# A window-attention layer and a dynamic convolution on one core: how the first rounds load their vectors and fold their weights

## The chip, the cores and the metric

The kernel runs on 1 core of one Trainium2 chip, in one launch. The metric is the device time of one execution in microseconds (us). Five engines work beside each other, each through its own queue in program order: TensorE (PE, matrix products into the banks called PSUM), VectorE (DVE), ScalarE (ACT), GpSimd (POOL), and SyncE (SP), which here only issues transfers (DMA). ACT can issue transfers too.

## The reference, cut to what matters

The input is 16 images of 192 channels, 56 x 56, in float32. Layer 0 is a shifted-window attention block (windows of 7 x 7, 6 heads of 32) with an MLP, layer 1 a 3 x 3 depthwise convolution whose taps are computed from the image's own mean.

```python
# layer 0
h = ln(x, norm1_g, norm1_b)                 # over the 192 channels of a pixel
win = windows(roll(h, (-3, -3)))            # (B*64, 49, 192)
q, k, v = split(win @ qkv_w + qkv_b)
attn = softmax(q * SCALE @ k.T + bias[rel] + mask)
x1 = x + unroll(attn @ v @ proj_w + proj_b)
y = gelu(ln(x1, norm2_g, norm2_b) @ fc1_w + fc1_b) @ fc2_w + fc2_b
x = x1 + y
# layer 1
t = relu(bn(x.mean((2, 3)) @ w1.T))
wt = (t @ w2.T + b2).reshape(B * 192, 1, 3, 3) * MASK   # four taps are left
out = depthwise_conv(x, wt) + bias
```

The normalisation's scale and shift need not be applied to the pixels. With g, b and the mean over channels, `ln(x) @ W + c = rstd * (x @ W') + (b @ W + c)`, where W' is W with its rows times g, and then less its column mean. The kernel computes W' (it is called centred) and `b @ W` (the shift) once, for the qkv weights and for the fc1 weights. This is called folding.

## The kernel before

**Tiling.** An image is cut into 4 strips (NU) of two bands of 7 rows, one band in partitions 0 to 63 and one in 64 to 127; the 192 channels are three groups (G) of 64. 16 images make S = 64 strips, and the index s of a strip is called a step here. A strip is two times 392 (UT) pixels wide. Weights are held twice, for the two halves of the partitions, where the contraction is over 64 channels.

**Rounds.** The program is written as rounds r from -2 to S + 2. A round works on several steps at once: scores and values of step r, q and k of step r + 1, the attention-weighted sum and the projection of step r - 1, the first MLP layer of step r - 2, the second of step r - 3, and pieces of the convolution of an image that is finished. In the first rounds (r < 3, called early) the statistics of the first normalisation come from a full product (`full_deviations`, PE L385), so that each is ready at once; later they go by a transfer to memory and back (`deviations`).

**Order.** No engine's order is written by hand. Each operation is handed to a planner (`Plan.add`) with its engine, a guessed duration, the keys that it reads and writes, a lag if it is a transfer, and sometimes a due time (`by`). PE's operations keep the order in which they are added. For the other engines the planner simulates the program with those guesses and takes, whenever an engine is free, the operation that can start first, and of those the one that is due first. So a guess, a key or a due time that is changed can move instructions on every engine but PE. Eight transfers at most are in flight: each issue, on SP or on ACT, waits for the one eight places before it.

**What the change touches.** Lines are those of the kernel before.

- `small_loads` (L1184): 14 transfers for the seven vectors of 192 numbers (`vecs`, one element to a partition, for both halves), six for the qkv biases (`qkb`, `bv`), one for `fc1_b` (`f1b`), all on ACT's queue, 21 in all.
- `load_qkv` (L1236): ten transfers on SP that put the qkv weights in the tile `wqkv`, in an order of columns that gives chunks of 128 (q of four heads, k of four heads, q and k of the other two) and then v.
- `fold_weights` (L1290): for n = 0 (qkv) or 1 (fc1), in this order on PE: the shift `b @ W` as products with one moving column (L1302), and the means (L1320); then on DVE the centring in place (L1335).
- `fold_qkv` (L1355): shifts in five chunks, then the biases `bq`, `qbs`, `km` of q and k and `bv` of v.
- `fold_proj` (L1374): v's bias is not added to v. Since the shares of a row sum to 1, it passes through to the projection, and this function multiplies `bv` by the projection's weights (PE L1382, L1386, one column each) and adds `proj_b`, giving `pbt`, which `biased_rows` (L749) adds to x on ACT.
- `statistics(n, s)` (L291): squares of the strip (ACT L297), then three groups added into one for x and for the squares (POOL L304, L306).
- `full_deviations` (L379): PE L385, ACT L393, DVE L400, ACT L407 and L411 give 1 / std of every pixel, `rb`.
- `scaled1(s)` (L418): x times `rb`, sorted into windows, in the tile `xs1` (POOL L427, L438). `queries_keys` (PE L471) and `values` (PE L665) read it.
- `queries_keys` evacuates q on ACT (L484, L508), k on DVE and ACT (L495, L518, L527). `scores` is PE L551 and DVE L577, L588. `values` copies out on ACT (L680), and eight transfers (L689) turn the copies.
- `weighted` is PE L718, with the o copies on ACT (L745) and DVE (L747). `projection` is PE L789 and L775, added to x by DVE (L817). `first_layer` is PE L828.
- `biases_of_positions` (L1418): seven transfers `relrows` (L1441) within memory, and four that read them back (L1455); DVE L1470 adds them to the masks.

The early rounds as they are added:

```python
        if r == -2:
            ...
            load(1, -80.0, 5.0)
            scaled_g()
            statistics(0, 0)
            full_deviations()
            fold_qkv()
        ...
        if r == 0:
            fold_fc1()
            fold_taps()
        if r == 1:
            fold_proj()
```

Of the kernel before, what the change touches and what calls it, by code (L numbers as in the profile page):

```python
# [14 lines left out]
G = 3  # L15
# [125 lines left out]
def tile_swin_then_dynamic_conv(  # L141
# [70 lines left out]
    tt = sb("tt", 128, 2, 48, TL)  # L212
    pt = sb("pt", 128, 2, 48, TL)
# [28 lines left out]
    qkb = sb("qkb", 128, 3)  # L242
# [6 lines left out]
    bv = sb("bv", 128, 2)  # L249
    pbt = sb("pbt", 128, G)  # L250
# [40 lines left out]
    def statistics(n, s):  # L291

        xv = rows(s).rearrange("p g r c -> p g (r c)")
        add(
            "ACT",
            1.2,
            lambda: nc.scalar.activation(sq, xv, AF.Square),  # L297
            X(s),
            ["sq"],
        )  # L300
        for k, src, keys in ((0, xv, X(s)), (1, sq, ["sq"])):
            f = fold[:, n, k]
            def go(src=src, f=f):
                nc.gpsimd.tensor_tensor(f, src[:, 0], src[:, 1], ALU.add)  # L304
            def go2(src=src, f=f):
                nc.gpsimd.tensor_tensor(f, f, src[:, 2], ALU.add)  # L306
            add("POOL", 1.0, go, keys, [("f", n, k)])
            add("POOL", 1.0, go2, keys + [("f", n, k)], [("f", n, k)])
# [108 lines left out]

    def scaled1(s):  # L418

        xv = rows(s)  # L420
        d = xs1
# [3 lines left out]
        for g in range(G):  # L425
            def go(g=g):
                nc.gpsimd.tensor_tensor(  # L427
# [5 lines left out]
            add("POOL", 0.95, go, X(s) + RB(0), [("xs1", g)])  # L433
        last = d[:, :, nf * N : UT].rearrange("p g (r c) -> p g r c", c=WS)
        rg = rv.rearrange("p (o r) c -> p o r c", o=1)
        for lo, hi, at in ((0, WS - SHIFT, IMG - WS + SHIFT), (WS - SHIFT, WS, 0)):
# [7 lines left out]
            add("POOL", 0.35, go, X(s) + RB(0), [("xs1", "w", lo)])  # L444

    def XS1(s):
        return [("xs1", g) for g in range(G)] + [
            ("xs1", "w", 0),
            ("xs1", "w", WS - SHIFT),
        ]  # L450
# [12 lines left out]
    def queries_keys(s, parts):  # L463
        d = xs1
        for i in parts:
# [14 lines left out]
            add("PE", 1.98, product, XS1(s) + ["wqkv"], [pk])  # L480
# [23 lines left out]
            else:  # L504
                for ab in range(2):
                    for h, lo, hi in ((0, 0, QL), (1, QL, N)):
# [8 lines left out]
                        add("ACT", 0.4, go, [pk, "qb", "qpad"], [("q2", ab, h)])  # L515
                for h in range(2):
# [8 lines left out]
                    add("ACT", 0.71, go, [pk, "qb", "mask2"], [("kbd2", 0, h)])  # L525
# [9 lines left out]
                    add("DVE", 0.58, go, [pk, "qb", "mask2"], [("kbd2", 1, h)])  # L535
# [110 lines left out]
    def values(s):  # L646

        n = 8 * G * TL  # L650
# [7 lines left out]
        for m in range(G):  # L658
            p, pk = bank()

            def product(m=m, p=p):
                for g in range(G):
                    for wh in range(2):
                        for ab in range(2):
# [3 lines left out]
                                xs1[P(ab), g, wh * 4 * N : (wh + 1) * 4 * N],  # L668
# [5 lines left out]
            add("PE", 0.99, product, XS1(s) + ["wqkv"], [pk])  # L674
            for b, n in ((0, TL), (1, N - TL)):
                def keep(m=m, p=p, b=b, n=n):
# [3 lines left out]
                    nc.scalar.copy(dst, src[:, :, :, TL * b : TL * b + n])  # L680
# [888 lines left out]
    for r in range(-2, S + 3):  # L1569
# [41 lines left out]
        if r == 1:  # L1611
            fold_proj()
# [131 lines left out]
```

## Time and profile before

| what | value |
|---|---|
| median of 3 runs | 2756.68 us (2754.64, 2756.68, 2763.43) |
| the profiled execution | 2756.27 us, its span 2754.5 us |
| busy share of the span | PE 98%, DVE 71%, ACT 61%, POOL 56% |
| first MLP product (L828) starts | 128.79 us |
| bytes moved by DMA | 239.62 MB, mean 87 GB/s |

The profile is of one execution. Its span runs from the first instruction to the last; the time of the execution is 1.8 us longer. A row of the profile names a line, an engine, the tiles written and read, and the count. In float32 a product on PE shows as two passes, so that L385, which is two instructions, shows as four. [...]

### The profile page before, as it was taken

How to read it: one execution, taken by the hardware profiler on the slowest of the kernel's cores; microseconds unless marked ns; L12 is line 12 of the kernel's file. 1: busy time of each engine (PE TensorE's matmuls, PEld its weight loads, DVE VectorE, ACT ScalarE, POOL GpSimd, SP SyncE). 2: the span in 40 equal slices, each digit the busy share in tenths (PEclk: the TensorE clock that was granted, in tenths of full speed). 3: DMA queues.
4: the chain of work that ended last, by engine and by line, in shares of the span. 5: the costliest groups of instructions: out<-in, count | busy, mean ns of one | idle time of the engine just before them, and what ended most of it. 6: DMA issues, size and time to landing. Idle time of an engine off the chain costs nothing.

```text
span 2754.5 us, 78133 instructions
## 1 busy us (share of the span) xinstructions
PE 2709.1 (98%) x32869; PEld 1670.9 (61%) x32869; DVE 1958.3 (71%) x3452; ACT 1682.4 (61%) x2788; POOL 1554.8 (56%) x1436
## 2 busy tenths in 40 slices
PE   7899999999999999999999999999999999999998
PEld 5566566566566566566566566566566566666654
DVE  5765876768677676876767777676876767767674
ACT  3656666656666566666666666575666666566553
POOL 5555565565565565565655655655655655655532
PEclk9899999999999999999999999999999999999999
DMA  6522353343424344253353423344253343533231
GB/s 128 111 63 60 72 119 71 80 101 91 105 67 100 73 99 94 68 127 67 74 109 87 109 67 90 77 104 92 67 122 74 76 109 70 115 79 71 62 78 52
DMA packets 146840, 239.62 MB, mean 87 GB/s; under 512 B 39432, under 2 KB 104888, under 8 KB 146488
## 3 DMA queue, kind: packets, MB, share of 16 engines
q1 hardware_dynamic: 141400, 233.40, 37.9%
q8 instruction: 258, 4.23, 0.7%
q10 hardware_dynamic: 5088, 1.22, 0.3%
q14 instruction: 94, 0.77, 0.1%
HBM read 66.81 MB, written 38.98 MB: 38 GB/s over the span
## 4 chain that ended last, share of the span: by engine, by line
PE 97%; DVE 1%; POOL 1%; ACT 0%; issue 0%; DMA 0%; ACTq 0%; DVEq 0%; POOLq 0%
PE ps L866 28%; PE ps L828 28%; PE ps L471 14%; PE ps L665 7%; PE ps L551 5%; PE ps L718 5%; PE ps L789 5%; PE ps L775 2%; PE ps L320 2%; PE ps L1302 0%; DVE sq L962 0%; POOL xs L427 0%; DVE hid L1142 0%; PE ps L1320 0%; PE ps L385 0%
## 5 line engine op out<-in xcount | busy, mean ns | idle before, releaser
L866 PE MATMUL ps<-hid,wf 128*64 128x392 f32 x4608 | 774.0, 494 | 0.3 <-issue 0.3
L828 PE MATMUL ps<-xs,wf 64*128 64x392 f32 x4608 | 769.5, 489 | 0.0
L828 PEld LDWEIGHTS ps<-xs,wf 64*128 64x128 f32 x4608 | 445.9, 187 | 312.6 <-issue 0.9
L866 PEld LDWEIGHTS ps<-hid,wf 128*64 128x64 f32 x4608 | 331.2, 137 | 406.6 <-issue 369.6
L304 POOL TENSOR_TENSOR fold<-sq 128x392 f32<-128x392 f32 x128 | 130.6, 1021 | 699.8 <-PE ps L320 690.0
L611 POOL TENSOR_TENSOR e<-e,tot 128x784 f32<-128x784 f32 x192 | 324.1, 1699 | 206.7 <-DVE tot L606 197.2
L840 ACT ACTIVATE hid<-ps,b1f 128x784 f32<-128x784 f32 x384 | 342.1, 913 | 141.2 <-PE ps L828 138.8
L471 PE MATMUL ps<-xs,wqkv 64*128 64x392 f32 x2304 | 407.6, 504 | 12.0 <-POOL xs L438 9.4
L1142 DVE SCALAR_TENSOR_TENSOR y<-x,wt,y 128x770 f32<-128x770 f32 x270 | 313.9, 1182 | 66.1 <-ACT y L1004 45.2
L471 PEld LDWEIGHTS ps<-xs,wqkv 64*128 64x128 f32 x2304 | 220.2, 190 | 178.4 <-issue 19.4
L593 POOL TENSOR_TENSOR e<-e,top 128x784 f32<-128x784 f32 x192 | 283.1, 1503 | 35.8 <-DVE top L588 35.8
L484 ACT ACTIVATE q<-ps,qbs 128x400 f32<-128x400 f32 (+1 forms) x128 | 68.3, 588 | 327.9 <-PE ps L471 327.9
L605 DVE TENSOR_REDUCE tot<-e 128x16 f32<-128x784 f32 x192 | 182.1, 948 | 109.9 <-ACT e L600 109.8
L745 ACT COPY o<-ps 32x392 f32<-32x392 f32 x512 | 243.8, 476 | 16.7 <-PE ps L718 3.0
L622 DVE STREAM_TRANSPOSE tt<-e 128x512 f32<-128x512 f32 x384 | 245.8, 684 | 3.0 <-POOL e L611 1.5
L756 ACT ACTIVATE x<-x,pbt 128x392 f32<-128x392 f32 x192 | 105.3, 612 | 204.8 <-POOL xs L438 204.8
L341 DVE TENSOR_TENSOR m<-ps,m 128x196 f32<-128x196 f32 (+1 forms) x64 | 23.2, 362 | 275.6 <-ACT m L334 275.5
L427 POOL TENSOR_TENSOR xs<-x,rb 128x343 f32<-128x343 f32 x192 | 186.7, 1001 | 39.0 <-DMA rb<-rsd 17.7
L456 POOL TENSOR_TENSOR xs<-x,rb 128x392 f32<-128x392 f32 x192 | 193.4, 1039 | 25.2 <-DMA rb<-rsd 25.2
L665 PE MATMUL ps<-xs,wqkv 64*64 64x196 f32 x4608 | 206.0, 328 | 0.7 <-DVE rb L400 0.3
L304 POOL TENSOR_TENSOR fold<-x 128x392 f32<-128x392 f32 x128 | 131.9, 1031 | 121.3 <-DVE x L817 92.9
L577 DVE TENSOR_TENSOR e<-ps,bt 128x784 f32<-128x784 f32 x192 | 175.2, 967 | 11.8 <-ACT hid L840 6.8
(128 smaller groups left out, 3649.8 us busy)
## 6 DMA issues: line engine op xcount, KB each, us to landing
pt<-tt SPq DMA_DIRECT2D x256, 192.0 KB
vb<-kbd SPq DMA_DIRECT2D x488, 96.0 KB
x<-in_x_dram SPq DMA_DIRECT2D x112, 294.0 KB
out_dram<-y SPq DMA_DIRECT2D x135, 196.0 KB
pt<-tt SPq DMA_DIRECT2D x256, 96.0 KB
rb<-rsd SPq DMA_DIRECT2D x118, 196.0 KB
out_dram<-y SPq DMA_DIRECT2D x45, 154.0 KB
x<-in_x_dram SPq DMA_DIRECT2D x16, 168.0 KB
```

Source lines behind the costliest of these rows:

```text
L304: nc.gpsimd.tensor_tensor(f, src[:, 0], src[:, 1], ALU.add)
L456: nc.gpsimd.tensor_tensor(xs2[:, g], xv[:, g], rb[:, 1], ALU.mult)
L471: nc.tensor.matmul(p[:, ab, 0:UT], lhs_qk(ab, g, i), d[P(ab), g, 0:UT], start=(g == 0), stop=(g == G - 1), tile_position=(64 * ab, 0),)
L593: nc.gpsimd.tensor_tensor(ev, ev, top[j].broadcast_to([128, 16, N]), ALU.subtract)
L611: nc.gpsimd.tensor_tensor(ev, ev, tot[j].broadcast_to([128, 16, N]), ALU.mult)
L622: nc.vector.transpose(tt[:, kb, 16 * j : 16 * j + 16], src)
L665: nc.tensor.matmul(p[P(wh), ab, 0 : 4 * N], wqkv[P(ab), g, 2 * DIM + 64 * m : 2 * DIM + 64 * m + 64], xs1[P(ab), g, wh * 4 * N : (wh + 1) ...
L745: add("ACT", 0.5, lambda dst=dst, src=src: nc.scalar.copy(dst, src), [k], [("o", j, i)])
L828: nc.tensor.matmul(p[:, ab, 0:UT], wf1[P(ab), g, f * 128 : (f + 1) * 128], xs2[P(ab), g], start=(g == 0), stop=(g == G - 1), tile_position ...
L840: nc.scalar.activation(hid[:, f], p[:, :, 0:UT], AF.Gelu, bias=b1f[:, f : f + 1])
L866: nc.tensor.matmul(p[P(ab), 0, 0:UT], wf2[:, f, g * 64 : (g + 1) * 64], hid[:, f, ab], start=(f == 0), stop=(f == NFC - 1), tile_position= ...
L1142: nc.vector.scalar_tensor_tensor(dst, s_, w[:, g, t : t + 1], dst, ALU.mult, ALU.add)
```

## The change

The vectors are loaded as rows of 64 or 128 numbers into two blocks of the tile `hid` that is still free (11 transfers on ACT's queue, due first), and each block is transposed by PE into columns (`small_columns`), from where DVE copies them into `vecs`, `qkvb` and `f1b`. The identity that this needs is made at the start.

The qkv weights are loaded into `wraw`, which is the tile `tt` before it is needed, and stay raw; the centred weights are written to `wqkv`, with keys of their own for q, for k with the third chunk, and for v. On PE the means come first. The shift of the first two chunks follows, that of the third comes after q and k of its first two chunks (`fold_qkv_rest`), and v's shift, now in the layout of v's copies, after the third (`fold_v`).

v's bias is added where ACT copies v out of PSUM; `fold_proj` and `pbt` are gone, and `biased_rows` adds `proj_b` itself. `fold_fc1` and `fold_taps` move from round 0 to round 1. Step 1's scaled rows go to `xs2` instead of `xs1`. The first strip's squares and their adds, and the third group of its scaled rows, go to DVE. The `relrows` transfers get a due time ahead of the second strip's load.

```diff
+    wraw = tt.rearrange("p b k t -> p (b k t)")[:, 0 : G * 3 * DIM]
...
+        first = n == 0 and s == 0
+        if first:
+            add("DVE", 1.3, lambda: nc.vector.tensor_tensor(sq, xv, xv, ALU.mult), X(s), ["sq"])
+        else:
+            add("ACT", 1.2, lambda: nc.scalar.activation(sq, xv, AF.Square), X(s), ["sq"])
...
+            eng, at, dur = ("POOL", nc.gpsimd, 1.0)
+            if first and k == 1:
+                eng, at, dur = ("DVE", nc.vector, 0.5)
...
+    def xs_of(s):
+        return (xs2, "xs2") if s == 1 else (xs1, "xs1")
...
+            if s == 0 and g == G - 1:
+                eng, at, dur = ("DVE", nc.vector, 0.5)
...
-            add("PE", 1.98, product, XS1(s) + ["wqkv"], [pk])
+            add("PE", 1.98, product, XS1(s) + [("wqkv", min(i, 1))], [pk])
...
-                    nc.scalar.copy(dst, src[:, :, :, TL * b : TL * b + n])
+                    src = src[:, :, :, TL * b : TL * b + n]
+                    nc.scalar.activation(dst, src, AF.Identity, bias=bv[:, m : m + 1])
...
-                    xv[:, m], xv[:, m], AF.Identity, bias=pbt[:, m : m + 1]
+                    xv[:, m], xv[:, m], AF.Identity, bias=vecs[:, 4, m : m + 1]
...
+        loads = [
+            (first, 0, 3, twice(norm1_g)),
+            (first, 3, 3, twice(norm1_b)),
+            (first, 6, 2, wide(qkv_b, 0, DIM, 2)),
+            (first, 8, 1, pairs),
+            (first, 9, 3, twice(qkv_b[2 * DIM :])),
+            (second, 0, 3, twice(norm2_g)),
...
+            (second, 15, NFC, wide(fc1_b, 0, 128, NFC)),
+        ]
+        for i, (t, lo, n, src) in enumerate(loads):
+            def go(t=t, lo=lo, n=n, src=src):
+                nc.scalar.dma_start(rows_of(t, lo, n), src)
+            add("ACT", 0.65, go, [], [("row", i)], lag=3.0, by=-99.0)
+    def small_columns(i):
...
+            lambda: nc.tensor.transpose(p[:, 0, 0:n], t[0:n], ident[0:n, 0:n]),
...
+    def fold_v():
+        p, pk = bank()
+        def go():
+            for m in range(G):
+                for g in range(G):
+                    for ab in range(2):
+                        nc.tensor.matmul(
+                            p[P(ab), ab, m : m + 1],
+                            wraw[P(ab), g, 2 * DIM + 64 * m : 2 * DIM + 64 * m + 64],
+                            vecs[P(ab), 1, g : g + 1],
...
-            add("SP", 0.4, go, [], [("relrows", yq)], lag=4.0)
+            add("SP", 0.4, go, [], [("relrows", yq)], lag=4.0, by=-85.0)
...
             load(1, -80.0, 5.0)
-            scaled_g()
+            small_columns(0)
             statistics(0, 0)
+            scaled_g(0)
             full_deviations()
             fold_qkv()
+            small_columns(1)
+            scaled_g(1)
...
-            queries_keys(r + 1, (0, 1, 2))
+            if r == -1:
+                queries_keys(0, (0, 1))
+                fold_qkv_rest()
+                queries_keys(0, (2,))
+                fold_v()
+            else:
+                queries_keys(r + 1, (0, 1, 2))
             full_deviations()
+        if r == 1:
+            fold_fc1()
+            fold_taps()
         if has(r - 1):
             weighted(r - 1)
-        if r == 0:
-            fold_fc1()
-            fold_taps()
-        if r == 1:
-            fold_proj()
```

## The prediction

> **What bounds the kernel now.** I read the page first, for where TensorE (PE) is not full.
>
> ```profile
> span 2754.5 us, 78133 instructions
> PE 2709.1 (98%) x32869; PEld 1670.9 (61%) x32869; DVE 1958.3 (71%) x3452; ACT 1682.4 (61%) x2788; POOL 1554.8 (56%) x1436
> PE   7899999999999999999999999999999999999998
> ```
>
> PE is full except in the first slices and the last. Then PE's busy time by long stretches (columns: stretch, length, busy, count, granted clock, DMA share, GB/s):
>
> ```profile
> 0.00:130.00 130.00, 99.54 (x1089) 0.88 0.57 123
> 130.00:700.00 570.00, 569.26 (x7062) 1.00 0.37 82
> 2732.00:2754.50 22.50, 12.13 (x42) 0.88 0.42 110
> ```
>
> The first 130 us hold 30.5 of the 45.4 us that PE stands idle, and a clock of 0.88. From there to 2732 us the four stretches leave only 5.7 us idle. The diff touches nothing after the first rounds, so the gain is how much earlier PE reaches its steady stream, whose first instruction is the first MLP product (L828). The chain of waits of the first 150 us gives the stations (start, length, what):
>
> ```profile
> 12.05 1.67 PE ps L385 x2
> 13.72 5.93 PE ps L1302 x30
> 19.66 4.20 PE ps L1320 x8
> 24.64 8.08 PE ps L471 x36
> ...
> 43.33 2.90 POOL xs L427 x3
> ...
> 54.61 4.11 PE ps L1302 x36
> 58.71 3.53 PE ps L1320 x10
> ...
> 70.27 2.89 POOL xs L427 x3
> ...
> 128.79 12.05 PE ps L828 x72
> ```
>
> L471 are the q and k products of steps 0, 1, 2, 3 (24.64, 46.90, 73.82, 107.61); values (L665) of steps 0 and 1 start at 39.15 and 67.24; the first projection (L775) ends at 97.7. I walk these stations again with the new order of each engine, which I read from the changed program (L1235, L1333, L1353, L1369, L1426 and L837 are lines of it), and durations from before.
>
> **Part by part.**
>
> *Rows, transposes, first statistics.* 21 column loads leave ACT's queue (0.6 to 0.75 us of issue each); 11 row loads come, of 1 to 6 runs of 256 or 512 bytes. In the waits of before, ACT reached its first squares at 8.64 after 4.5 us behind such loads. Now DVE does this square and its two adds. DVE's nearest row with both inputs in SBUF is L1470: a 294-wide and a 98-wide take 0.84 together, the latter 0.31, so 1.13 ns per element and 0.2 fixed: square (1176) 1.53, adds (392) 0.64 each. x lands at 6.9 as before. POOL adds x meanwhile (2 x 1.01). By these rows the last add ends at 9.7, instead of 12.0, PE's L387 pair (1.67 each) at 12.4 instead of 13.7.
>
> [...] beside each other, these took 1.44 instead of 1.01, and 1.03 instead of 0.53:
>
> ```profile
> 33.66 1.44 POOL L304 TENSOR_TENSOR fold<-x 128x392 f32<-128x392 f32 x1 [7.24 <-PE ps L385]
> 37.47 1.03 DVE L1470 TENSOR_TENSOR bt<-hid 128x294 f32<-128x294 f32 x1
> ```
>
> [...] But what follows needs the qkv weights, whose tenth issue ran at 11.47 to 12.1 and comes no more than a microsecond sooner (the first waits for a row load, the fifth for a later one); PE read the last of them after 13.65 without a stall. I start L1353 at 13.7 either way[...].
>
> *Raw weights apart.* Means (L1353) 13.7 + 4.2 = 17.9; then only 12 of 30 one-column passes (5.93 / 30 = 0.198) 2.4, and the second transpose 0.3 (three took 0.5): q starts at 20.6. Ready by then: scaled rows (rb chain 0.50 on ACT, 0.57 on DVE, 0.62 and 0.53 on ACT with hops 2.4 after L387, POOL 2 x 0.98 + 0.64, DVE its third beside them: by 19.5) and centred columns (three of 128, 0.34 each by L1335's 410 ns for 192 and 611 for 384: by 19.0). Gain 4.0.
>
> *v's bias.* L1426 adds 36 passes behind q and k; fold_proj's 24 took 3.13, so 4.7. Values of step 0: 20.6 + 8.1 + 0.7 (six shift passes left) + 4.7 + 1.5 (L387) + 2.5 (scores) = 38.1. The evacuation that PE waited for at 36 to 38 (in step 1 its last piece, L508, ended 5.1 after q and k, at 58.2) ends at 29.4 + 5.1 = 34.5, hidden under L1426. Gain only 1.05: the added passes pay for it. The bias in the ACT copies I cost at nothing: as many instructions, and the copy rows (0.28 to 0.37) lie near ACTIVATE's (0.40 for 64x192); ACT has slack there.
>
> *Step 1's rows in xs2.* POOL waited 13.8 us in total for values to leave xs1 (L427 from PE L665, twice). Now step 1 waits for rb alone: L387 ends 35.6, square 0.5, DVE's subtraction behind one score evacuation until 37.9, Ln and Exp to 39.1, POOL 3.55: q of step 1 at 42.7 (before 46.90). Gain 4.2.
>
> *fc1 folded a round later.* Step 1 loses 8.6 us of PE (L1302, L1320, L1527) and DVE's six L1335 (3.24), which kept scores waiting 1.8. New cover: 42.7 + 6.2 + 1.5 + 1.6 is 52.0, the evacuation ends at 48.9 + 5.1 = 54.0; third scores and a bank: values of step 1 at 55.3, end 58.3. POOL must by then have step 2's rows: three subtracts (4.4) and a fold to 48.1, three multiplies to 52.6, fold of x(3), rows (rb ready at about 54) to 57.6. So q of step 2 at 58.3 (before 73.82), without PE's wait and so at 6.2 where it took 9.08 with 5.9 of it at half clock (0.50 to 0.58 in the trace from 74 to 80): 64.5, L387 66.0. Then fc1's fold 8.6 to 74.6 (its ACT-wait cover kept), weighted 2.5 to 77.1. Late next: the DVE queue. L1369 (3.24) starts at 74.2 and stands ahead of the o copies (2.25): 79.8. PE waits 2.7 there. fold_proj's 3.13 are gone, but they had covered the ACT copies. Projections 4.1 + 1.5 at half clock as before: 85.4 (before 97.7). Gain 12.3.
>
> *Steps 2 to 3.* POOL's order (fold of step 0, rows of step 3) and DVE's stay: I keep 128.79 - 97.7 = 31.1. L837 at 116.5.
>
> *Queues.* On SP, seven relrows issues (5.8 us) pass ahead of x(1): issued at 17 to 18.5 instead of 12.7 to 14.2, landing by 24.5 (before it took at most 5.75). ACT's square of x(1) ends at 25.7 and stands before q's evacuation, whose bank L1426 needs at 29.4: 2.6 us of cover. Half of x(3) goes behind eight value copies: issued about 48, landing about 53 where POOL comes at 52.6; rb covers that. Position biases: on DVE behind the k evacuation, data by 26.
>
> The sum: 12.3 off the profiled run's 2756.27 (span 2754.5 and 1.8 around it) is 2744.0. The median of the three runs is 0.4 higher, less than they differ (2754.64 to 2763.43).
>
> **The clock.** After one-column passes the clock falls though PE counts as busy:
>
> ```profile
> 88.00:90.00 2.00, 1.97 (x43) 0.98 1.08 245
> 90.00:92.00 2.00, 2.00 (x15) 0.50 0.34 74
> ```
>
> By that row L1426 would put L387, scores and values of step 0 at half speed: 3 us more than in my walk (which has 3.0 for values, before 4.05). [...] The range takes 3 us either way from this.
>
> **Rivals.** About 0.3% (8.3 us) is what a measurement of this kernel can tell from no change.
> - *The added passes[...] eat it*: L1426 at the cold 0.198 (7.1, +2.4), the clock after it (+3)[...]: gain 5.9, 2750.4. For: both rows above. Against: step 1's waits fall away later and absorb some. Chance 0.20.
> - *The clock stays up*: denser work, projections at 1.99 (their steady length) instead of 4.1, step 3's q at 6.2 instead of 9.25: 5 more, 2739. [...] Against: the waits at 79.8 and before step 3 remain. Chance 0.16.
> - *Slower*: x(1) behind relrows. Their 49 short runs each, if slow, hold x(1); its square blocks ACT, q's bank and L1426. It costs from a landing at 27.1 on, eats the gain at 39.4, loses 0.3% at 48. For: SP's seven issues did take 5.8. Against: relrows went out in the same way before, and x(2) behind them came in time. Chance 0.03: 2765.
> - *Not as it says*: rows landing late would move the first transpose, but PE has nothing before 9.08 and columns landed at 6.96; no effect.
>
> **How the numbers follow.** The forecast (gain 8.3 to 15) 0.61, clock 0.16, eaten 0.20, slower 0.03: faster 0.77, same 0.20, slower 0.03. Range 2735 to 2752: clock with its 3 us below, eaten with 1.5 above.
>
> **What would show it.** L837 starts near 116.5; q of steps 0 to 2 near 20.6, 42.7, 58.3; no POOL wait on PE at step 1; a wait of PE for o copies near 78; DVE's square beside POOL's adds 1.5 or 2.5. Wrong if q of step 0 starts after 23, if values of step 0 are later than before, or if PE shows new idle time after 130.

## The result, and the profile after

The changed kernel takes 2751.79 us (median of 22 runs, 2747.70 to 2754.92), the kernel before in the same sessions 2758.18. The ratio is 0.9976, with a 95% interval of 0.9969 to 0.9982: a gain of 6.4 us, where the forecast had 12.3. The profiled execution took 2753.09 us, 3.2 less than the profiled one of before; so the two profiles are closer than the medians, and I read them for the first 130 us, where the stations are, and not for the difference of their spans.

The page, and PE's busy time by long stretches (stretch, length, busy of each engine, granted clock as a share of full speed, DMA share, GB/s):

```profile
span 2750.9 us, 78130 instructions
PE 2705.4 (98%) x32871; PEld 1664.0 (60%) x32871; DVE 1965.7 (71%) x3462; ACT 1717.9 (62%) x2787; POOL 1552.8 (56%) x1433
PE   7899999999999999999999999999999999999998
```
```profile
0.00:130.00 130.00, 102.60 (x1137) 69.57 (x1139) 89.47 (x176) 64.75 (x119) 77.52 (x84) 0.84 0.58 126
130.00:700.00 570.00, 568.90 (x7080) 349.76 (x7078) 402.69 (x720) 363.38 (x590) 331.88 (x304) 1.00 0.36 81
```

In the first 130 us PE is idle for 27.4 us instead of 30.5, so less of the idle time went than the stations moved. The clock of this row, 0.84 against the 0.88 of before, is not a fair comparison: the rows of before say 1.00 from 9 to 28 us, although two passes of L385 take 1.67 us there (12.05) and four take 1.58 later (32.65), so a pass took twice as long there. From 28.5 us to the first MLP product the clock is 0.85 before and 0.82 after; by that the clock took a part back. The chain of waits of the first 150 us (start, length, what):

```profile
18.14 4.68 DMA x<-in_x_dram
...
38.77 4.37 PE ps L673 x72
...
55.57 3.65 PE ps L673 x48
...
60.03 0.99 DVE e L584
...
61.16 6.20 PE ps L478 x36
...
68.86 4.81 PE ps L1333 x36
73.68 4.13 PE ps L1353 x10
...
79.14 3.24 DVE wf L1369 x6
...
100.23 7.19 PE ps L478 x24
...
121.31 12.05 PE ps L837 x72
```

| station (us) | before | forecast | after | a second profile of after |
|---|---|---|---|---|
| q and k of step 0 (L478) | 24.64 | 20.6 | 18.11 | 18.10 |
| values of step 0 (L673) | 39.15 | 38.1 | 38.54 | 37.99 |
| q and k of step 1 | 46.90 | 42.7 | 43.02 | 42.43 |
| values of step 1 | 67.24 | 55.3 | 55.57 | 54.98 |
| q and k of step 2 | 73.82 | 58.3 | 61.16 | 60.56 |
| end of the first projection (L784) | 97.7 | 85.4 | 90.4 | 89.8 |
| first MLP product (L837) | 128.79 | 116.5 | 121.25 | 120.63 |

The second profile of after is that of e12 below. The first q came 2.5 us sooner than forecast; from the values of step 0 to those of step 1 the walk holds within half a microsecond; then it loses 4.7 us, nearly all of it ahead of the end of the first projection. From the waits of PE in the first 135 us (who waited for whom, us in total, times, longest):

```profile
PE ps L558 <- ACT q L515: 6.5, 2, 4.3
...
PE ps L478 <- POOL xs L447: 4.1, 2, 2.9
...
PE ps L727 <- DVE wf L1369: 1.8, 1, 1.8
...
PE ps L798 <- DVE w1t L1579: 1.0, 1, 1.0
PE ps L478 <- DVE e L584: 1.0, 1, 1.0
```

The wait for POOL before step 1 is gone, and the new wait for the o copies is there with 2.8 us (L727 behind DVE's L1369, L798 behind the last of DVE's queue). The first row was not forecast with this size.

### The profile page after: what moved, and what is told of

It is laid out like the page before. It is cut to its first block, busy times and chain, and to the rows that moved or that the text cites. A ratio compares the mean times of both kernels' runs of the same rounds, so it can differ in the third digit from the quotient of the medians.

```text
span 2750.9 us, 78130 instructions
## 1 busy us (share of the span) xinstructions
PE 2705.4 (98%) x32871; PEld 1664.0 (60%) x32871; DVE 1965.7 (71%) x3462; ACT 1717.9 (62%) x2787; POOL 1552.8 (56%) x1433
## 3 DMA queue, kind: packets, MB, share of 16 engines
q8 instruction: 258, 4.23, 0.7%
## 4 chain that ended last, share of the span: by engine, by line
PE 95%; DVE 2%; SPq 1%; DMA 1%; issue 0%; ACT 0%; POOL 0%; ACTq 0%; DVEq 0%
PE ps L875 28%; PE ps L837 28%; PE ps L478 13%; PE ps L673 7%; PE ps L558 5%; PE ps L798 5%; PE ps L727 5%; PE ps L784 2%; PE ps L322 2%; DVE trow L970 0%; DVE hid L1151 0%; DVE x L826 0%; DVE sq L971 0%; SPq L1174 0%; DMA wf<-in_L_conv_fc_w_dram 0%
## 5 line engine op out<-in xcount | busy, mean ns | idle before, releaser
L837 PE MATMUL ps<-xs,wf 64*128 64x392 f32 x4608 | 769.5, 489 | 0.0
L837 PEld LDWEIGHTS ps<-xs,wf 64*128 64x128 f32 x4608 | 445.9, 187 | 312.6 <-issue 0.9
L478 PE MATMUL ps<-xs,wqkv 64*128 64x392 f32 x2304 | 406.9, 502 | 7.2 <-POOL xs L447 4.1
L478 PEld LDWEIGHTS ps<-xs,wqkv 64*128 64x128 f32 x2304 | 220.2, 189 | 171.4 <-issue 20.1
L765 ACT ACTIVATE x<-x,vecs 128x392 f32<-128x392 f32 x192 | 105.8, 615 | 209.4 <-POOL xs L447 209.4
L673 PE MATMUL ps<-xs,wqkv 64*64 64x196 f32 x4608 | 206.8, 329 | 2.2 <-issue 1.9
L436 POOL TENSOR_TENSOR xs<-x,rb 128x343 f32<-128x343 f32 x191 | 186.3, 1004 | 30.8 <-DMA rb<-rsd 21.2
L673 PEld LDWEIGHTS ps<-xs,wqkv 64*64 64x64 f32 x4608 | 173.6, 134 | 18.1 <-issue 3.0
```

Source lines behind the costliest of these rows:

```text
L478: nc.tensor.matmul(p[:, ab, 0:UT], lhs_qk(ab, g, i), d[P(ab), g, 0:UT], start=(g == 0), stop=(g == G - 1), tile_position=(64 * ab, 0),)
L673: nc.tensor.matmul(p[P(wh), ab, 0 : 4 * N], wqkv[P(ab), g, 2 * DIM + 64 * m : 2 * DIM + 64 * m + 64], xs[P(ab), g, wh * 4 * N : (wh + 1) * ...
L837: nc.tensor.matmul(p[:, ab, 0:UT], wf1[P(ab), g, f * 128 : (f + 1) * 128], xs2[P(ab), g], start=(g == 0), stop=(g == G - 1), tile_position ...
```

## The experiments

All times are medians; the last column compares each with the kernel before on the same chip. The runs were made on several chips, so rows are compared by their ratios. The start of L837 is read from one execution of each kernel.

| kernel | L837 starts | us (before beside it) | ratio, 95% interval |
|---|---|---|---|
| changed | 121.25 | 2751.79 (2758.18) | 0.9976, 0.9969 to 0.9982 |
| changed, again (e12) | 120.63 | 2747.09 (2756.17) | 0.9968, 0.9958 to 0.9979 |
| changed, step 1 in xs1 (e8) | 128.60 | 2753.06 (2753.41) | 0.9998, 0.9988 to 1.0007 |
| before, step 1 in xs2 (e9) | 123.42 | 2749.44 (2756.17) | 0.9974, 0.9965 to 0.9983 |
| changed, first strip back (e10) | 118.76 | 2747.37 (2756.17) | 0.9966, 0.9954 to 0.9978 |
| changed, fc1 back (e4) | 119.14 | 2748.31 (2755.77) | 0.9971, 0.9961 to 0.9981 |
| changed, km first (e1) | 120.69 | 2747.10 (2755.77) | 0.9965, 0.9953 to 0.9977 |
| changed, wide shift (e2) | 118.97 | 2745.53 (2755.77) | 0.9956, 0.9941 to 0.9971 |
| changed, split fold (e3) | 122.08 | 2748.90 (2755.77) | 0.9971, 0.9962 to 0.9979 |
| the three together (e5) | 114.89 | 2743.46 (2753.41) | 0.9964, 0.9950 to 0.9977 |
| and late loads (e6) | 110.63 | 2741.40 (2753.41) | 0.9954, 0.9941 to 0.9966 |
| and warm products (e7) | 111.92 | 2739.16 (2753.41) | 0.9944, 0.9931 to 0.9958 |
| and loads spread (e11) | 111.20 | 2736.50 (2756.17) | 0.9928, 0.9914 to 0.9942 |

### Which part carries the gain

**e8: step 1's rows back in xs1.**

```diff
-        return (xs2, "xs2") if s == 1 else (xs1, "xs1")
+        return (xs1, "xs1")
```

> Starting from the changed kernel: step 1's scaled rows go to xs1 again, as before. Theory A (the forecast: the second buffer is worth the wait for POOL, 3.6 us at step 1): q and k of step 1 start 3.6 us after the values of step 0 end, at about 46.7 instead of 43.0, and everything up to L837 (121.25) is 3 to 3.6 us later. Theory B (later waits absorb it: q and k of step 1 wait less for what follows, and the waits of 2.2 for q's pieces at step 1 and 1.0 before step 2 shrink): q of step 2 is later by less than 2 us and L837 by less than 1.5. A third case: the clock; one more idle stretch of 3.6 us costs a half-clock stretch of 3.4 or 6.8 us, and L837 is later by 5 or more.

Measured: L837 at 128.60, 7.3 later, and the time of the kernel before to a part in a thousand. (The profiled execution took 2762.92, the longest of the fourteen; the median is 2753.06.) The third case is what happened. From PE's timeline (start, length, line, count, idle before it and its releaser):

```profile
45.49 7.89 PE L478 MATMUL ps<-xs,wqkv 64*128 64x392 f32 x36 [3.66 <-POOL xs L447]
65.50 7.89 PE L478 MATMUL ps<-xs,wqkv 64*128 64x392 f32 x36 [3.06 <-POOL xs L447]
74.83 5.84 PE L1333 MATMUL ps<-vecs,wf 64*128 64x1 f32 x36
```

Each wait of 3 us for POOL is followed by products that take 7.89 instead of 6.20, and the fold of fc1 starts 6.0 us later than in the changed kernel (68.80). Each stall costs its own length and 1.7 us more in the products behind it, as 3.4 us at half clock would (the profile of after has stretches of 3.41 and 6.83 us at 0.50: 55.01 to 58.42, 72.07 to 78.90); waits further on give a part of that back. Both waits, ahead of step 1 and of step 2, are back, although fc1's fold has stayed in round 1.

**e9: the kernel before with step 1 in xs2, and nothing else.**

```diff
-        d = xs1
+        d, name = (xs2, "xs2") if s == 1 else (xs1, "xs1")
...
-        d = xs1
+        d = xs2 if s == 1 else xs1
...
```

> Starting from the kernel before: only step 1's scaled rows go to xs2 instead of xs1; nothing else of the change. The changed kernel without this one edit had its first MLP product at 128.60 us, as the kernel before (128.79), and the same time. Theory A (the second buffer alone carries the gain, the rest of the change is worth nothing): q and k of step 1 start right behind the values of step 0 (before: 46.90), L828 about 7 us earlier (121.5), and the time 6 us under that of the kernel before, as with the whole change. Theory B (the parts need each other: without the earlier q of step 0 and with fc1's fold at step 1, POOL or the fold decides): q and k of step 1 gain 2 to 3.5 us, the values of step 1 as much, but L828 gains under 4 us and the time 1 to 3 us.

Measured: 0.9974, the same gain as the whole change; L829 (the first MLP product there) at 123.42 is 5.4 earlier than before, between the two theories, and the time says A. With e8, from the other side, this settles it: one edit, which the forecast credited with 4.2 us at one station, carries the measured gain. The rest of the change together adds nothing that these runs can tell (0.9976 and 0.9968 against 0.9974); on this chip the medians of e9 and e12 are 2.4 us apart, within the intervals, so a microsecond or two may be hidden there. q and k of steps 1 and 2, first in the kernel before, then here:

```profile
46.90 6.20 PE L471 MATMUL ps<-xs,wqkv 64*128 64x392 f32 x36 [3.09 <-POOL xs L438]
73.82 9.08 PE L471 MATMUL ps<-xs,wqkv 64*128 64x392 f32 x36 [3.41 <-POOL xs L438]
```
```profile
44.72 6.20 PE L472 MATMUL ps<-xs,wqkv 64*128 64x392 f32 x36
68.72 6.20 PE L472 MATMUL ps<-xs,wqkv 64*128 64x392 f32 x36 [0.47 <-DVE e L578]
```

Step 1 starts with no wait. Step 2 no longer waits for POOL either, since xs1 is free for its rows, and its products take 6.20 instead of 9.08, with fc1's fold still in round 0. The forecast had put the end of that second wait down to the fold's move.

**e10: the first strip's square, adds and third group back on ACT and POOL.**

```diff
-        first = n == 0 and s == 0
+        first = False
...
-            if s == 0 and g == G - 1:
+            if False:
```

> Starting from the changed kernel: the first strip's square goes back to ACT, its two adds and the third group of its scaled rows back to POOL. In the changed kernel DVE's square took 1.37, its adds 1.26 (beside POOL's add, which took 2.10 instead of 1.0) and 0.57, and the second L387 pair started when POOL's add ended. Theory A [...]: L387 ends 1 us later than in the changed kernel (12.76), the scaled rows 2 us later (18.07: three groups on POOL), q of step 0 at 20 to 21 instead of 18.1, and L837 (121.25) 1 to 2 us later. Theory B (what follows does not wait for it: ACT's evacuation of step 0, which waited for km, sets the scores): q of step 0 is later by 2 us, values of step 0 by less than 0.5, and L837 and the time stay within 1 us of the changed kernel's.

Measured: the L387 pair ended at 12.9 instead of 12.7, q of step 0 started at 19.59 instead of 18.11, the values of step 0 at 38.19 (38.54), and L837 and the time are not later. Theory B. In the changed kernel the square on DVE took 1.37 and the add beside it on POOL 2.10, where the next ones take 1.02:

```profile
7.49 1.37 DVE L297 TENSOR_TENSOR sq<-x 128x1176 f32<-128x1176 f32 x1
7.62 2.10 POOL L308 TENSOR_TENSOR fold<-fold,x 128x392 f32<-128x392 f32 x1
24.08 1.02 POOL L308 TENSOR_TENSOR fold<-fold,x 128x392 f32<-128x392 f32 x1
```

Beside the square, POOL's add took 1.1 us longer, and the edit is left with 0.2 us at L387.

L837 is even 2.5 earlier here (118.76), for another reason. The shift and the means of fc1's fold, which this edit leaves alone, in the changed kernel and in e10:

```profile
68.80 4.88 PE L1333 MATMUL ps<-vecs,wf 64*128 64x1 f32 x36
73.54 4.35 PE L1353 MATMUL ps<-wf,gs 64*128 64x384 f32 x10
```
```profile
68.62 4.18 PE L1333 MATMUL ps<-vecs,wf 64*128 64x1 f32 x36
72.66 3.96 PE L1353 MATMUL ps<-wf,gs 64*128 64x384 f32 x10
```

The whole fold takes 8.6 us in e10, as in the kernel before, where the clock is at half for 3.4 of them (0.82 from 54 to 63.5), and 10.2 in the changed kernel, with 6.8 (0.50 from 72.07 to 78.90). So the same fold came at two prices, and a difference of 2 us in L837 between two single profiles shows nothing by itself.

**e4: fc1's fold and the taps back in round 0.**

```diff
-        if r == 1:
-            fold_fc1()
-            fold_taps()
         if has(r - 1):
             weighted(r - 1)
+        if r == 0:
+            fold_fc1()
+            fold_taps()
```

> Starting from the changed kernel: fc1's fold and the taps' transposes go back to round 0 (behind the weighted sums, where they were). Theory A (the forecast's account: at step 1 the fold costs 8.6 us in front of q and k of step 2; in round 1 it costs the same and a wait for the o copies of 2.8, and covers 2 to 3 us of waiting for ACT): the two places come out within 1.5 us of each other at L837 (121.25), q and k of step 2 start near 68 instead of 61.2. Theory B (moving it was a gain of its own): L837 is later by 3 us or more. Theory C (moving it was a loss: in round 0 it fills a time in which PE waits anyhow, in round 1 it runs at half clock and causes a wait): L837 is earlier by 2 us or more.

Measured: q and k of step 2 at 66.16, L837 at 119.14, the time as that of the changed kernel. C by L837 (2.1 earlier, which is within what e10 shows), A by the time. The fold took 8.6 us in round 0 and 10.2 in round 1; with the fold in round 0, PE then waits 3.61 and 2.63 us ahead of and within L798, for the o copies of ACT and of DVE. PE's wait ahead of q and k of step 2 is 0.47, so the fold's move was not what took the wait for POOL away. Moving the fold was worth nothing that these runs can tell.

**e12: the changed kernel again.**

> The changed kernel itself, unaltered, beside the three others. By the 22 runs on record its ratio to the kernel before is 0.9976 (0.9969 to 0.9982). Its profile is a second sample of one execution: L837 was at 121.25 in the first. Theory A [...]: the stretches of half clock lie elsewhere, q of step 0 takes between 4.2 and 7.3 for its first two chunks, and L837 differs by 1 to 3 us. Theory B (they are fixed by the program): the same stretches within 0.5 us and L837 at 121.3.

Measured: 0.9968, and L837 0.6 earlier. Theory A at step 0, where the first two chunks of q and k took 4.22 us instead of 7.26 in the same program (from 17 to 23 us the clock is 1.00 here and 0.54 in the first profile); but the waits behind them, up to the values of step 0, absorbed 2.5 of the 3.0 us, and from 50 us on the instructions that run slow are mostly the same. So between these two executions the clock at step 0 moved a station by 3 us and L837 by 0.6; by e10 it can be more.

### Where the forecast's other 4.7 us went

**e2: 160 columns in fc1's shift (n = 1) instead of one.**

```diff
+                    o = p[0 : a.shape[1], 0, c : c + 1]
+                    b_ = vecs[0:64, 2 * n + 1, g : g + 1]
+                    if n == 1:
+                        o = p[:, c // 3, 160 * (c % 3) : 160 * (c % 3) + 160]
+                        b_ = b_.broadcast_to([64, 160])
                     nc.tensor.matmul(
-                        p[0 : a.shape[1], 0, c : c + 1],
+                        o,
                         a,
-                        vecs[0:64, 2 * n + 1, g : g + 1],
+                        b_,
...
```

> Starting from the changed kernel: the 36 one-column passes of fc1's shift (L1333 in fold_fc1) get a moving operand of 160 equal columns instead of one, [...] the result is read from every 160th column. Theory A [...]: the granted clock from 72 to 79 goes from 0.50 to 1.00, the 12 passes of the means (L1353, from 73.5 to 79.0) take about 2.2 us instead of 5.5, and L837 starts 3 us earlier (118.3); the time 2749. Theory B (the clock falls for another reason, for instance the waits before): the clock stays at 0.50 there, the fold stays at 10.3 us or grows with the longer passes (36 times up to 0.07, 2.5 us), and the time is the same or up to 2 us longer.

Measured, in the stretch of the fold, first the changed kernel, then this one:

```profile
72.00:79.00 7.00, 7.00 (x24) 4.85 (x23) 3.77 (x7) 2.16 (x4) 4.80 (x4) 0.51 0.61 136
```
```profile
72.00:79.00 7.00, 7.00 (x101) 6.01 (x99) 5.85 (x12) 3.49 (x8) 5.43 (x4) 1.00 0.51 115
```

PE is busy for all of the 7.00 us in both; the clock is 0.51 with one column and 1.00 with 160. The 36 passes take 5.22 instead of 4.88, the fold 7.8 instead of 10.2. In the six executions with one column and the fold in round 1 (the changed kernel twice, e1, e3, e8, e10) the first ten passes of the means took 3.96 to 4.37 us; in the five with 160 columns (e2, e5, e6, e7, e11) they took 2.20 to 2.31. Theory A's clock is what was measured: with one-column passes in this fold the clock falls although PE counts as busy, and with 160 columns in the same passes it does not. Why, no run shows. L837 is 2.3 earlier, although q of step 0 was 1.3 later in this execution; by the time (0.9956) e2 cannot be told from e12 (0.9968).

**e3: the shift ahead of the weighted sums, the means and the centring behind them.**

```diff
+    def centre_fc1():
...
         if r == 1:
             fold_fc1()
-            fold_taps()
         if has(r - 1):
             weighted(r - 1)
+        if r == 1:
+            centre_fc1()
+            fold_taps()
```

`fold_fc1` keeps the shift alone; `centre_fc1` has the means and the centring.

> Starting from the changed kernel: in round 1 the shift of fc1 (L1333) stays ahead of the weighted sums of step 0 (L727), and the means, the centring and the taps' transposes (L1353, DVE L1369, L1569) come behind them, ahead of the projection. So the o copies stand ahead of the 3.24 us of centring in DVE's queue. Theory A (the wait that the forecast named is real and costs what it measures, 1.8 us of L727 on DVE L1369 and 1.0 of L798 on DVE): both waits go, the projection's end moves from 90.39 to about 87.6 and L837 from 121.25 to 118.5. Theory B (the wait covered another): the time goes to the next wait, for instance L727 on ACT's q pieces (L515) or L798 on ACT's o copies, and L837 moves by less than 1 us. Theory C (clock): the means run at half clock in the new place as well, so the gain is there but the fold still takes 10 us.

Measured: both waits went. From the start of the fold to the end of the first projection it is 17.5 us instead of 21.6. But L837 is at 122.08, later than in the changed kernel, since PE stands in the values of step 2:

```profile
89.65 1.70 PE L673 MATMUL ps<-xs,wqkv 64*64 64x196 f32 x33
94.84 3.54 PE L673 MATMUL ps<-xs,wqkv 64*64 64x196 f32 x39 [3.49 <-issue]
```

It waits for no semaphore that the profile shows. The changed kernel stood at the same instruction for 0.28 and went on at 94.42, e2 for 2.45 and went on at 94.56. What is won before is lost here.

**e1: km's operations ahead of the mask adds.**

```diff
-        add("DVE", 0.4, biases, [pk, "mask2", "qkvb"], ["qb2"])
+        add("DVE", 0.4, biases, [pk, "mask2", "qkvb"], ["qb2"], by=-50.0)
```

> Starting from the changed kernel: the DVE operations that make km and the third chunk's bias (L1410 to L1412) get a due time ahead of the seven mask adds (L1513, 3.1 us) that stood before them. By the trace of after, ACT waited 4.9 us for km (L525 from DVE L1412), PE waited 4.3 us for ACT (second part of the scores of step 0, from 31.5 to 35.87). Theory A (a DVE queue order sets step 0, not the 36 passes of L1426, which took 1.2 instead of 4.7): PE's wait there falls under 1.5 us, values of step 0 start near 35.5 (38.54), q and k of step 1 near 40 (43.02), and the first MLP product (L837, 121.25) 2 to 3 us earlier; the time 2749. Theory B (the forecast's reading: PE's own work sets the station at 38.1): values of step 0 stay at 38 and nothing moves. Theory C (the clock takes it back): step 0 is earlier by 3 us but L837 by less than 1, with more half-clock time between 40 and 120.

The wait that it is about, in the changed kernel: DVE's timeline, and PE's.

```profile
27.44 3.07 DVE L1513 TENSOR_TENSOR bt<-hid 128x294 f32<-128x294 f32 x7
30.43 0.15 DVE L1410 TENSOR_TENSOR bq<-ps,qkvb 128x1 f32<-128x1 f32 x1
```
```profile
27.95 1.21 PE L1426 MATMUL ps<-vecs,tt 64*64 64x1 f32 x36
...
35.87 2.89 PE L558 MATMUL ps<-kbd,q 64*64 64x98 f32 x64 [4.33 <-ACT q L515]
```

Measured: L1412, which makes km, starts at 27.7 instead of 30.8, but eight of the mask adds (28.87 to 33.65) then stood ahead of DVE's L534, and PE waited 2.71 for that. From q of step 0 to the values of step 0 it is 18.4 us instead of 20.4; L837 is 0.6 earlier, the time not distinguishable from the changed kernel's. Theory A for the cause, and a miss for the size: the same queue holds the next wait.

**e5: the three together.**

> Starting from the changed kernel: the three edits together (km's bias operations ahead of the mask adds, 160 columns in fc1's shift, the means and the centring behind the weighted sums). Theory A (the three costs are separate: 0.8 of DVE's order, 2.5 of the clock in the fold, 2.8 of the wait for the o copies): the first projection ends near 84 (90.39 in the changed kernel), q and k of step 3 (100.23) near 95 and L837 (121.25) near 116; the time about 0.4% under that of the changed kernel. Theory B (a later bound holds the gain back): in the runs of the wide shift and of the split fold, PE stood for 2.45 and 3.49 us in the middle of the values of step 2 with nothing that the profile names (issue), and went on at 94.56 and 94.84 in both, as in the changed kernel at 94.42, although it had come there 2 us earlier. In each, a packet of 16 KB on the queue of kind instruction had landed 1.5 us before (92.9 to 93.4), sent when the DMA engines, full since 76 with nine loads of x, came free. By B the stall grows with every microsecond won before it: PE resumes at 94.5 again, q and k of step 3 stay near 99 and L837 near 118.5.

Measured: the first projection ends at 81.2, L837 is at 114.89. Both theories have their share: 9.2 us are won up to the projection, 2.8 of them are lost in the stretch behind it. PE stood in the values of step 2 for 2.50 us and went on at 87.84, not at 94.5: the stall moves with the stream.

```profile
87.84 2.42 PE L673 MATMUL ps<-xs,wqkv 64*64 64x196 f32 x38 [2.50 <-issue]
```

### What bounds it next

**e6: as e5, and the loads of x from step 5 on behind the shares of step 1.**

```diff
-            add("SP", 0.2 * (hi - lo), go, writes=[("x", b % 3, u, h) if lo == 0 else ("x", b % 3, u, 2)], lag=lag, by=by)
+            add("SP", 0.2 * (hi - lo), go, ["sent1"] * (s > 4), [("x", b % 3, u, h) if lo == 0 else ("x", b % 3, u, 2)], lag=lag, by=by)
...
             turn_shares()
+            if r == 1:
+                plan.writer["sent1"] = plan.writer[("pt", 2, 1, 1)]
```

> As the kernel with the three edits together, and the loads of x from step 5 on (nine of 126 to 294 KB, issued one after the other from 74 to 81) wait in SP's order until the shares of step 1 are sent. Theory A (the stall in the values of step 2 is the instruction packet behind those loads): the DMA share from 76 to 90 falls from 1.0 to under 0.5, the packet lands before PE needs it, the stall of 2 to 5 us in the values of step 2 goes, and q and k of step 3 start at the end of the values of step 2 plus 3.9 (POOL's rows), near 95; L837 near 116. Theory B (the stall is something of PE's own, not of the DMA): it stays, and PE resumes at 94.5. Either way the loads may come too late for step 5 (its rows are squared at about 120): then a wait for x shows after L837.

Measured: the stall is gone, q and k of step 3 start at 89.89 and L837 at 110.63, earlier than either theory had. Of the 4.3 us against e5, 1.3 stood already at q of step 2 (58.72 against 59.97), ahead of the loads that the edit moves; and the times of e5 and e6 cannot be told apart. The DMA share of 80 to 100 fell to 0.49, from 0.93 in e5. For 76 to 92, first e2, which has the same loads as e5, then this one:

```profile
76.00:92.00 16.00, 12.35 (x283) 10.04 (x281) 14.06 (x33) 5.16 (x10) 3.17 (x4) 0.89 0.97 205
```
```profile
76.00:92.00 16.00, 12.62 (x243) 8.92 (x241) 15.05 (x32) 7.68 (x15) 9.59 (x12) 1.00 0.30 65
```

A packet of 16 KB on the queue of kind instruction went out between 79.8 and 80.0, as PE began the 96 passes of L558 (80.02); in e2 none went out from 80 to 91, though PE had begun them at 88.18, and one did between 91.5 and 93. Those 96 passes and the 32 to 34 of L673 up to the stall are, with a weight load each, 256 to 260 instructions, if every pass and every load counts as one. The profile's page of after has for the whole execution 32871 passes, as many weight loads, and 258 such packets (4.23 MB), which would be 255 to a packet, if all packets were PE's (an estimate from these counts):

```profile
q8 instruction: 258, 4.23, 0.7%
```

So I read the stall as a wait of PE for its next instructions; what a packet holds, no run shows. It lasted over 2 us where those passes go by in 4 us (81.26 to 85.35 in e5) with the DMA share near one: 2.45 us in e2 (0.97), 2.50 in e5. In the changed kernel a packet went out at 91.60 and landed at 92.91, and PE, after its 0.28, went on at 94.42, 1.5 us after that; for e2, e3 and e7 the expectations of e5 and e11 have 1.5 us too. The loads put off met the next such packet: 1.26 us of stall at 130.81, behind a packet that went out at 128.26 and took 1.25, so that it landed near 129.5.

**e7: as e6, and 32 product passes (16 products) that nobody reads, while PE has nothing to do before 9.8 us.**

```diff
+    def warm(n, keys):
+        def go():
+            for _ in range(n):
+                nc.tensor.matmul(ps[3][:, 0, 0:128], full, full, start=True, stop=True)
...
+            warm(8, ["blk"])
             small_columns(0)
+            warm(8, [])
```

> As the kernel before with late loads, and 16 products of 128 by 128 that nobody reads are put on PE while it has nothing to do (8 ahead of the first transpose at 6.3, 8 behind it, from about 2 to 9.7 us). Theory A (the half clock of the first rounds is PE's own idle time before 9.77): the granted clock is 1.00 from about 6 on, the first L387 pair takes 1.6 instead of 2.98, L1353 2.2 instead of 2.86 to 4.2, q and k of the first two chunks of step 0 4.2 instead of 7.0, and q of step 0 starts near 17; values of step 0 2 to 3 us earlier, L837 by 1 to 2 us. Theory B (what waits behind it takes it back: the qkv weights land at about 12.7, the scaled rows of step 0 at 18 and ACT's evacuation decide): L387 is faster, but q of step 0 starts at 17.5 to 18 and L837 moves by less than 1 us.

Measured: L387 took 2.29 from 10.22 instead of 2.98 from 9.77, q of step 0 started at 17.85 (18.10), and its first two chunks took 5.92. Theory B: the scaled rows set the start, and the clock was 0.66 from 18 to 23 us. L837 is no earlier than in e6.

**e11: as e7, but the late loads spread over steps 1 to 3.**

```diff
-            add("SP", 0.2 * (hi - lo), go, ["sent1"] * (s > 4), [("x", b % 3, u, h) if lo == 0 else ("x", b % 3, u, 2)], lag=lag, by=by)
+            add("SP", 0.2 * (hi - lo), go, [f"sent{min((s - 3) // 2, 3)}"] * (s > 4), [("x", b % 3, u, h) if lo == 0 else ("x", b % 3, u, 2)], lag=lag, by=by)
...
-            if r == 1:
-                plan.writer["sent1"] = plan.writer[("pt", 2, 1, 1)]
+            plan.writer[f"sent{r}"] = plan.writer[("pt", 2, 1, 1)]
```

> As the kernel with all edits and the warm products, but the late loads of x are spread: those of step 5 follow the shares of step 1, those of steps 6 and 7 the shares of step 2, the next two steps those of step 3. With the loads put off in one block, the DMA share was 0.9 from 100 to 130 and PE stood for 1.28 us (issue) at 131.12, 1.5 us after an instruction packet had landed. Theory A (the packet waits where the loads are): the share from 100 to 130 falls to about 0.6 and the 1.3 us stall near 130 goes; L837 stays near 112, the time 1 us under 2739. Theory B (the stalls named issue come of their own): a stall of over 1 us between 120 and 140 stays, and the time is the same.

Measured: the stall near 130 is gone, and the time is 2736.50: 0.9928 of the kernel before, 0.9914 to 0.9942, beside 0.9968 of the changed kernel on the same chip. First the stretch with the loads in one block (e6; e7 has a DMA share of 0.91 there), then this one:

```profile
100.00:130.00 30.00, 25.23 (x355) 17.27 (x355) 19.40 (x38) 22.41 (x36) 17.98 (x17) 0.89 0.89 187
```
```profile
100.00:130.00 30.00, 25.46 (x364) 17.54 (x368) 19.51 (x39) 21.66 (x35) 17.41 (x16) 0.89 0.48 103
```

It has the lowest ratio of the kernels here; its interval just overlaps that of e7 (0.9931 to 0.9958), and lies below that of e5 (0.9950 to 0.9977).

## Why the prediction was right or wrong

- **The outcome.** The sign, and the place where the gain would show, were right; the median lies at the upper end of the range, and the size was half of what was forecast. Two things are in the gap: L837 came 4.7 us later than forecast, and the gain at the end was 6.4 of the 7.5 at L837. The second is no more than such profiles scatter: PE idles 4.6 us from 130 to 2732 us before and 7.7 after, in pieces mostly named issue, at lines that the diff doesn't touch, and the 13 kernels' gains at the end lie within about 6 us of their gains at L837.
- **The step that failed** is the walk from the values of step 1 to the end of the first projection: 30.1 us forecast (55.3 to 85.4), 34.8 measured (55.57 to 90.39). Four terms make the 4.7 us: fc1's fold (1.6), the values of step 1 (1.6), a wait ahead of step 2 (1.0) and the weighted sums (0.7); the others cancel. Three of the four are half clock (0.50 from 72.07 to 78.90, from 55.01 to 58.42 and from 82.31 to 89.14). The walk took it out of q and k of step 2, rightly (6.20 instead of 9.08), and let it come back only in the projection. From the values of step 0 to the end of the first projection the trace has, first before, then after:

```profile
39.15:97.70 58.55, 48.15 (x551) 33.76 (x555) 46.39 (x68) 30.00 (x62) 30.61 (x28) 0.83 0.59 132
```
```profile
38.54:90.39 51.85, 45.80 (x534) 32.49 (x529) 40.04 (x60) 28.93 (x59) 31.53 (x29) 0.81 0.64 138
```

  Taken as time at 1.00 and time at 0.50, this is about 20 us at half in both (an estimate from these rows): it moved to other products and did not get less.
- **fc1's fold** was put at 8.6 us because it took that in round 0, with 3.4 us of it at half clock. It took 10.2 in round 1, with 6.8 us at half clock, and 7.8 in e2, with none (1.00 from 68 to 79): with one column in its shift the clock fell, with 160 it did not. In e10 it took 8.6 in round 1 as well, so the old price was one of the prices it can have. The prediction had the clock of 0.50 from 90 to 92 us, behind one-column passes, but used it for L1426 alone and left the fold at its old price.
- **Values of step 1** were put at 3.0 us and took 4.59, with the clock at half from 55.0 to 58.4: they follow a wait of 2.16 us for q's pieces. In e6 and e11 the same wait stood there and the clock stayed up; what decides it is open. So is the half clock in the second part of the weighted sums (1.61 us for 32 passes; 0.92 in e2), which took 3.2 in all where the walk had 2.5.
- **Ahead of step 2**, a wait of 0.99 for DVE's L584 was not in the walk (no run was made to take it away).
- **L1426 (v's bias)** was put at 4.7, with 7.1 in the rival. It took 1.21. The station behind it still came out right (38.54 for 38.1), because PE then waited 4.33 for ACT, and ACT for km behind seven mask adds on DVE: a right number by a wrong reason. The rest of the scores and the values of step 0 ran at half clock behind that wait (0.50 from 34.53 to 41.36; 64 passes of L558 in 2.89 us; 1.59 at step 1), which the prediction had in its range and not in its walk. The order of DVE was to be read from the changed program, and I had placed km behind the k evacuation alone.
- **The first strip.** L387 ended earlier than forecast and the means of the qkv weights started at 12.7, not 13.7; q of step 0 was set by POOL's rows (18.07). 2.5 us better than forecast there, and worth nothing: the wait of 4.33 absorbed it (in e10 q starts 1.5 later, and the values of step 0 no later).
- **Step 1's rows.** The wait for POOL fell as described and q of step 1 came at 43.02 for 42.7. But the forecast credited the parts one after the other, and credited the fold's move with most of the rest. e8 and e9 show that the order of the sum hid the ownership: the second buffer also ends the wait ahead of step 2 (3.41 before, 0.47 for DVE in e9) and the slow products behind it (9.08 before, 6.20 in e9), and alone gives the gain that was measured. That the sum came near the stations up to step 1 owes something to errors that cancelled (see L1426).
- **The new wait** for the o copies: forecast 2.7, measured 2.8. Half-clock projections: forecast 5.6, measured 5.35. The last stretch: forecast 31.1, measured 30.9. The loads of x(1): landing by 24.5 forecast, 22.8 measured.
- **The rivals.** The one whose time was nearest (2750.4, the added passes) fell by its causes: the passes took 1.2 us, not 7.1, and the 1.1 us of POOL's add beside DVE's square delayed nothing that counted (its 5.9 has a further microsecond for DVE and POOL beside each other, an estimate). Its term for the clock after such passes was real in fc1's fold (0.51); that its time came near is luck. The clock that stays up was not the changed kernel's, but e11's: 1.00 from 40 to 100 us and L837 at 111.20.
- **A slip in the working:** the four stretches from 130 to 2732 us leave 4.6 us of idle time, not 5.7. Nothing rests on it.

## What to carry to other kernels

Price each part of a bundle alone, from both ends: here a second buffer for one step, tried by itself, gave the measured gain, and undoing it left nothing. When the start of a kernel is made denser, look for what the freed time turns into: here a clock that fell in a fold with one-column products although PE counted as busy (0.51; 1.00 with 160 columns, e2), and instruction packets that went out late beside bulk loads which nobody needed yet (a stall of 2.45 us at a DMA share of 0.97 in e2, none in the same place at 0.30 in e6). Putting such loads off, in small lots, ended the stalls of over a microsecond here (e11); what that alone is worth in time these runs cannot tell, only that with the warm products it took the ratio from 0.9964 (e5) to 0.9928 (e11).

## What was not expected of the hardware

- In fc1's fold, with one-column products in its shift, the clock fell while PE was 100% busy (0.51 from 72 to 79 us, against 1.00 with 160 columns, e2).
- The 36 one-column passes of L1426, on 64 x 64 weights at two places of the array in turn, took 34 ns each; the 36 of L1333, on 64 x 128 weights at one place, 116 to 136 ns. No run tells which of the two differences does it.
- PE stood for up to 3.5 us (e3) with loads of x on the DMA engines and an instruction packet still to land, and the profile names it only as issue; with the loads put off the stall was gone (e6).
- The clock that the profile shows for the first microseconds does not fit the products there: the rows of before say 1.00 from 9 to 28 us, where two passes of L385 take 1.67 us and four take 1.58 later.
